# Layer norm by 32x32 tiles, a searched order for the attention and another step for Sobel, in a four-layer network

## The chip, the cores and the metric

The kernel runs on one core of one Trainium2 chip. Its time is device microseconds from start to end of one execution, given as a median of several runs. One execution is also recorded by the hardware profiler; PE is the matrix engine, PEld its weight loads, DVE the vector engine, ACT the scalar engine, POOL the GpSimd engine, and SP a queue that only issues DMAs.

## The reference

The input x is 256 x 256 positions of 32 channels, f32. Four layers follow, each `x = x + f(gn(x))`, where gn is a group norm over the whole picture (16 groups of 2 channels) without weights.

```
layer 0: mn = (m - mean) * rsqrt(var + eps) * gamma + beta     # over the 32 channels
         o  = sigmoid(mn @ Wg) * (mn @ Wv)                     # 32 -> 256
         return o @ Wo + bo                                    # 256 -> 32
layers 1, 2: pooled = 3x3 mean; sqrt(sobel_x(pooled)^2 + sobel_y(pooled)^2 + 1e-6)
layer 3: two recurrent cells of width 128 with group norm, over 256 steps of 256 sequences
```

In layer 0 the softmax is summed over the axis on which it was normalised, so that factor is 1 and queries and keys drop out; the kernel computes the two matmuls, the gate and the projection alone.

## The kernel before

The picture lies in SBUF as `xa`, 128 partitions x 64 blocks x 256: partition = position within a block (4, called j) x 32 channels, free = 256 rows. Work goes by pairs of blocks, 128 x 512 numbers; there are 32 pairs (`NST`), and `pair(t, k)` is pair k of tile t. `xb` is a second tile of the same shape.

**Input** (L205 to L222): 16 loads of 512 KB on SP's queue, 4 transposes a pair on PE, a copy on ACT (L221), bn_stats on DVE (L222). Three buffers of x hold two loads each. Then `group_norm` (L156) makes scale and bias of each partition by two small matmuls, with filler matmuls between.

**Layer norm, first half** (L262 to L276). For each pair PE multiplies `xa` by a centring matrix `cen` that also holds the group norm's scale (L264), ACT squares the result (L266), and DVE writes it, plus the constant `cb`, to `xb` (L267). Groups of four squares are averaged over the channels by 32-column matmuls into one bank, `pvar` (L254). One square root (L274) and one reciprocal (L276) give `rstd`, a row for each j and pair.

**Layer norm, second half** (L282 to L300). For each pair PE spreads its rows of `rstd` over the partitions (L285), DVE multiplies (L292), and ACT or POOL in turn applies gamma and beta (L294, L298).

**Attention** (L314 to L382). Each pair needs 16 matmuls (L324) with 32 rows of weights, 128 columns and 512 moving columns: two halves (u) x four j, for values and for gates; j chooses the strip of 32 rows. ACT takes the sigmoid of a gate (L339), DVE multiplies it with the value into a tile `o` (L342, 17 buffers). `project` runs 8 matmuls with all 128 rows and 32 columns into one bank (L348), ACT adds the output's bias (L356), POOL adds to `xa` (L358), and DVE takes bn_stats (L361). Values and gates have four PSUM banks each. The order is written out: `together` takes four values or gates of four different j, and the projection of a pair follows one pair later. In `manual_schedule` every engine keeps the order in which the program issues.

`RecurrentWeights` (L618) loads the cells' weights `wc` (2 x 512 KB) and `bc` on SP's queue; `centring` (L659) is a list of small DVE and POOL instructions on them, spread over the attention's pairs.

**Sobel** (L393), twice. For each pair: `convert` (ACT, L451), `twos` (DVE, L455), `threes` (DVE, L470), `ends` (ACT, L460), `fours`, `difference`, `smooth` (POOL, L475, L483, L479), two `mixed` of PE (L517), two `square` (ACT, L523), `total` (DVE, L527), `root` (ACT, L531), `residual` (DVE, L534), `statistics` (DVE, L537). Each part has a due time in `parts`; part p of pair k is due at `k * every + when`, and the parts are issued in the order of their due times. So `every` sets the order on each queue, not a time.

**Recurrence** (L840): 256 steps, from 604 us to the end.

The functions around the change, with the line numbers that the profile uses:

Of the kernel before, what the change touches and what calls it, by code (L numbers as in the profile page):

```python
# [18 lines left out]
S = 256  # L19
T = 256  # L20
# [41 lines left out]
def net_kernel(  # L62
# [69 lines left out]
    wg4 = four_times(w_g, D, "wg4")  # L132
    wo = cp.tile([P, D // P, C], F32, name="wo")
# [21 lines left out]
    def group_norm(stats, psum, before, after, rhs=None):  # L155
# [22 lines left out]
        return scale, bias  # L178

    KS = NST // 4  # L180


    means = ExitStack()
    mp = means.enter_context(tc.tile_pool(name="means", bufs=1))
    avg = mp.tile([P, KS, KS, J], F32, name="avg")
    nc.gpsimd.memset(avg, 0.0)
    for ks in range(KS):
        nc.gpsimd.tensor_copy(avg[:, ks, ks, :], kt[:, K_AVG, 0:P:C])
    spread = mp.tile([P, KS * J, C], F32, name="spread")
    for g in range(4):  # L190
        rows = slice(g * C, (g + 1) * C)
        nc.gpsimd.tensor_copy(
            spread[rows], ident[rows, rows].unsqueeze(2).to_broadcast([C, KS * J, C])
        )
# [6 lines left out]
    with tc.tile_pool(name="nat", bufs=3) as natp, tc.tile_pool(  # L201
# [3 lines left out]
        for w0 in range(0, T, WL):  # L205
            nat = natp.tile([P, 2, WL, C], F32, name="nat")
            for h in range(2):
                nc.sync.dma_start(out=nat[:, h], in_=x_nat[:, h, w0 : w0 + WL, :])
            for b2 in range(WL // (2 * J)):
# [14 lines left out]
        gn = group_norm(stats, ps_in, 3, 2, xa[:, NB - 1, :])  # L224

# [4 lines left out]

    pairs = [(g * KS + ks, g, ks) for ks in range(KS) for g in range(4)]

# [3 lines left out]
    with tc.tile_pool(name="ln", bufs=4) as lnp:  # L239
        rstd = lnp.tile([P, 2 * S], F32, name="rstd", bufs=1)  # L240
        with tc.tile_pool(name="ps_ln", bufs=6, space=PSUM) as ps_ln, tc.tile_pool(
            name="ps_var", bufs=1, space=PSUM
        ) as ps_var:
            cen = lnp.tile([P, P], F32, name="cen", bufs=1)
            nc.vector.tensor_scalar(cen, kg[:, K_CEN, :], gn[0], None, ALU.mult)
            pcb = ps_var.tile([P, 1], F32, name="pcb")
            nc.tensor.matmul(pcb, lhsT=kg[:, K_CEN, :], rhs=gn[1], start=True, stop=True)
            cb = lnp.tile([P, 1], F32, name="cb", bufs=1)
            nc.vector.tensor_copy(cb, pcb)
            pvar = ps_var.tile([P, 2 * S], F32, name="pvar")  # L250
            sqs = {}

            def variance(k, g, ks):
                nc.tensor.matmul(  # L254
                    pvar[g * C : (g + 1) * C, :],
                    lhsT=avg[:, ks].rearrange("p k j -> p (k j)"),
                    rhs=sqs.pop(k),
                    start=ks == 0,
                    stop=ks == KS - 1,
                )  # L260

            for i, (k, g, ks) in enumerate(pairs):  # L262
                pc = ps_ln.tile([P, 2 * S], F32, name="pc")
                nc.tensor.matmul(pc, lhsT=cen, rhs=pair(xa, k), start=True, stop=True)  # L264
                sqs[k] = lnp.tile([P, 2 * S], F32, name="sq", bufs=10)
                nc.scalar.activation(sqs[k], pc, AF.Square, bias=cb)  # L266
                nc.vector.tensor_scalar(pair(xb, k), pc, cb, None, ALU.add)  # L267
                if g == 3 and ks:
                    for q in pairs[i - 7 : i - 3]:
                        variance(*q)  # L270
            for q in pairs[-4:]:
                variance(*q)
            std = lnp.tile([P, 2 * S], F32, name="std", bufs=1)
            nc.scalar.activation(std, pvar, AF.Sqrt, bias=ln_eps)  # L274
            table(AF.Sigmoid, std[:, 0:1])
            nc.vector.reciprocal(rstd, std)  # L276
            for _ in range(9):
                nc.tensor.matmul(
                    pvar[:, 0:S], lhsT=ident, rhs=kg, start=True, stop=True
                )  # L280
        with tc.tile_pool(name="ps_sp", bufs=8, space=PSUM) as ps_sp:
            for i, (k, g, ks) in enumerate(pairs):  # L282
                rows = slice(g * C, (g + 1) * C)
                pb = ps_sp.tile([P, 2 * S], F32, name="pb")
                nc.tensor.matmul(  # L285
                    pb,
                    lhsT=spread[rows, ks * J : (ks + 1) * J, :].rearrange("p j c -> p (j c)"),
                    rhs=rstd[rows, :],
                    start=True,
                    stop=True,  # L290
                )
                nc.vector.tensor_mul(pair(xb, k), pair(xb, k), pb)  # L292
                if i % 2:
                    nc.scalar.activation(  # L294
                        pair(xb, k), pair(xb, k), AF.Identity, scale=gamma4, bias=beta4
                    )
                else:
                    nc.gpsimd.tensor_scalar(  # L298
                        pair(xb, k), pair(xb, k), gamma4, beta4, ALU.mult, ALU.add
                    )  # L300
            junk = ps_sp.tile([P, 2 * S], F32, name="pb")
            for _ in range(4):
                nc.tensor.matmul(
                    junk[:, 0:S], lhsT=ident, rhs=kg, start=True, stop=True
                )
# [4 lines left out]
    cells = ctx.enter_context(tc.tile_pool(name="cells", bufs=1))  # L310
    rw = RecurrentWeights(tc, cells, w_cell, b_cell)
    centring = rw.centring()
    stats = new_stats()
    with tc.tile_pool(name="at", bufs=3) as atp, tc.tile_pool(  # L314
        name="ps_g", bufs=4, space=PSUM
    ) as ps_g, tc.tile_pool(name="ps_v", bufs=4, space=PSUM) as ps_v:
        gates, gated = {}, {}

        def inner(w, u, j, ps):
            i, half = divmod(u, 2)  # L320
            k = pairs[i][0]
            rows = slice(j * C, (j + 1) * C)
            mn = xb[rows, 2 * k : 2 * k + 2, :].rearrange("p b s -> p (b s)")
            nc.tensor.matmul(  # L324
                ps, lhsT=w[rows, half * P : (half + 1) * P], rhs=mn, start=True, stop=True
            )
            return ps

        def together(values, gates_of):

            pvs = {k: inner(wv4, *k, ps_v.tile([P, 2 * S], F32, name="pv")) for k in values}
            pgs = {
                k: inner(wg4, *k, ps_g.tile([P, 2 * S], F32, name="pg"))
                for k in gates_of
                if k[0] < 2 * NST
            }
            for k, pg in pgs.items():
                gates[k] = sg = atp.tile([P, 2 * S], F32, name="sg", bufs=8)
                nc.scalar.activation(sg, pg, AF.Sigmoid)  # L339
            for k, pv in pvs.items():  # L340
                gated[k] = o = atp.tile([P, 2 * S], F32, name="o", bufs=17)
                nc.vector.tensor_mul(o, pv, gates.pop(k))  # L342

        def project(i):
            po = ps_g.tile([P, 2 * S], F32, name="pg")
            for half in range(2):
                for j in range(J):
                    nc.tensor.matmul(  # L348
                        po[j * C : (j + 1) * C, :],
                        lhsT=wo[:, half, :],  # L350
                        rhs=gated.pop((2 * i + half, j)),
                        start=half == 0,
                        stop=half == 1,
                    )
            r = atp.tile([P, 2 * S], F32, name="r", bufs=2)
            nc.scalar.activation(r, po, AF.Identity, bias=bo4)  # L356
            dst = pair(xa, pairs[i][0])
            nc.gpsimd.tensor_add(dst, dst, r)  # L358

        def statistics(i):  # L360
            nc.vector.bn_stats(stats[:, i, :], pair(xa, pairs[i][0]))  # L361

        with tc.manual_schedule():
            together((), [(0, j) for j in range(J)])
            together((), [(1, j) for j in range(2)])
            for i in range(NST):
                for u in (2 * i, 2 * i + 1):
                    if i >= 3 and u % 2:
                        statistics(i - 3)
                    together([(u, 0), (u, 1)], [(u + 1, 2), (u + 1, 3)])  # L370
                    together([(u, 2), (u, 3)], [(u + 2, 0), (u + 2, 1)])
                if i >= 1:
                    project(i - 1)
                if centring:
                    centring.pop(0)()
            for part in centring:
                part()
            table(AF.Sqrt, one)
            for i in range(NST - 1, NST):
                project(i)  # L380
            for i in range(NST - 3, NST):
                statistics(i)  # L382
# [740 lines left out]
```

## Time and profile before

| | |
|---|---|
| median of 3 runs | 2561.74 us (2558.74 to 2562.13) |
| profiled execution: time | 2562.2 us |
| profiled execution: span from first to last instruction | 2560.4 us |
| granted PE clock, mean | 0.991 |
| PE, DVE, ACT, POOL busy | 98%, 89%, 88%, 51% |

The stages, read from the first instructions of each: input to 34.9 us, group norm to 38.8, layer norm to 101.2, attention from 102.2 to 322.6, Sobel to 455.9 and to 592, and the recurrence from 604.

The page counts an engine as busy from start to end of each instruction, and for PE the end of a pass is modelled, so a full PE column need not be a full PE. Idle time is put down to the instruction that ended it. A group's line gives the line, the engine, the operation, output<-inputs, the shapes, the count, then busy us and the mean ns of one, then idle time before it. A line of the timeline gives start, length, engine, line, operation and count; the length covers all instructions of that line of the answer.

### The profile page before, as it was taken

To read this page: it belongs to the slowest core of one execution; us is meant where nothing else is said; L and a number is where in the kernel's file an instruction comes from. 1 tells how busy PE (TensorE), PEld (TensorE's weight loads), DVE (VectorE), ACT (ScalarE), POOL (GpSimd) and SP (SyncE) were. 2 spreads that over 40 slices of the span, in tenths; PEclk is the share of its full clock that TensorE was granted. 3 is DMA by queue.
4 is the path that set the end of the run, shared out by engine and by line. 5 is a ranking of instruction groups with operands and counts; after the bars stand their busy time and mean duration, and the time that the engine had idled before them with its cause. 6 is when DMAs were issued, how large, how long until landed. Compare 5 with 4: busy or idle time off the path is not lost.

```text
span 2560.4 us, 41317 instructions
## 1 busy us (share of the span) xinstructions
PE 2506.6 (98%) x11469; PEld 1048.9 (41%) x11469; DVE 2266.8 (89%) x6667; ACT 2247.8 (88%) x6888; POOL 1315.4 (51%) x1356
## 2 busy tenths in 40 slices
PE   7999999998999999999999999999999999999997
PEld 4433344544444444444444444444444444444442
DVE  6788877775999999999999999999999999999997
ACT  5677766575999999999999999999999999999997
POOL 3222277673555555555555555555555555555553
PEclk9899999998999999999999999999999999999998
DMA  4000000002010101010101010000101010100000
GB/s 150 17 1 1 1 1 1 1 1 50 5 21 5 21 5 22 5 22 5 22 5 22 5 24 10 19 18 9 22 5 22 5 22 5 22 5 5 5 5 11
DMA packets 110872, 38.57 MB, mean 15 GB/s; under 512 B 74868, under 2 KB 107797, under 8 KB 110632
## 3 DMA queue, kind: packets, MB, share of 16 engines
q1 hardware_dynamic: 108452, 34.54, 6.2%
q8 instruction: 94, 1.54, 0.3%
q14 instruction: 146, 1.20, 0.1%
q10 hardware_dynamic: 1380, 0.99, 0.1%
q0 software_dynamic: 800, 0.30, 0.0%
HBM read 10.63 MB, written 8.39 MB: 7 GB/s over the span
## 4 chain that ended last, share of the span: by engine, by line
PE 88%; DVE 6%; ACT 2%; issue 2%; DMA 1%; POOL 0%; SPq 0%; POOLq 0%; DVEq 0%; ACTq 0%
PE zz L941 36%; PE zz L936 17%; PE zz L909 9%; PE pt L993 5%; PE pv L324 5%; PE zz L906 3%; PE pg L348 2%; PE pt L989 2%; PE pg L517 2%; ACT pg L531 1%; PE px L1038 1%; DVE pp L470 1%; PE pg L324 1%; DVE ss L527 1%; DVE u L455 1%
## 5 line engine op out<-in xcount | busy, mean ns | idle before, releaser
L957 POOL TENSOR_TENSOR rs<-ve,mhalf 128x4 f32<-128x4 f32 x1024 | 1031.9, 1008 | 925.1 <-DVE ve L954 925.1
L941 PE MATMUL zz<-wc,hT 128*128 128x512 f32 x2040 | 1059.4, 607 | 0.7 <-DVE hT L999 0.7
L930 ACT ACTIVATE ga<-zz,rs 128x128 f32<-128x128 f32 x3072 | 975.6, 378 | 38.7 <-POOL rs L957 10.2
L954 DVE TENSOR_REDUCE ve<-sq 128x4 f32<-128x516 f32 x1024 | 705.0, 688 | 29.5 <-ACT sq L949 8.5
L949 ACT ACTIVATE sq<-zz 128x512 f32<-128x512 f32 x1024 | 632.2, 617 | 37.4 <-PE zz L941 16.1
L936 PE MATMUL zz<-wc,hT 128*128 128x512 f32 x1024 | 525.0, 594 | 0.0
L941 PEld LDWEIGHTS zz<-wc,hT 128*128 128x128 f32 x2040 | 328.8, 190 | 399.1 <-DVE c L985 167.6
L930 ACT ACTIVATE go<-zz,rs 128x128 f32<-128x128 f32 x1024 | 395.0, 386 | 0.0
L977 DVE TENSOR_TENSOR c<-ga 128x128 f32<-128x128 f32 x1024 | 300.2, 293 | 62.5 <-ACT ga L930 29.8
L985 DVE TENSOR_TENSOR c<-c,fc 128x128 f32<-128x128 f32 x1020 | 288.5, 283 | 9.0
L981 DVE TENSOR_TENSOR fc<-ga,c 128x128 f32<-128x128 f32 x1020 | 292.5, 287 | 2.7 <-ACT ga L930 2.7
L909 PE MATMUL zz<-fx,xt 32*128 32x512 f32 x2048 | 266.0, 589 | 0.0
L342 DVE TENSOR_TENSOR o<-pv,sg 128x512 f32<-128x512 f32 x256 | 158.2, 681 | 39.7 <-PE pg L324 34.6
L993 PEld LDWEIGHTS pt<-ident,c 128*128 128x128 f32 x512 | 71.1, 139 | 286.0 <-DVE c L985 277.0
L996 ACT ACTIVATE th<-c 128x128 f32<-128x128 f32 x512 | 166.7, 326 | 0.4 <-DVE c L985 0.4
L339 ACT ACTIVATE sg<-pg 128x512 f32<-128x512 f32 x256 | 138.6, 599 | 31.6 <-PE pg L324 26.8
L517 PE MATMUL pg<-dh,kt 128*64 128x512 f32 (+1 forms) x584 | 156.5, 542 | 7.4 <-POOL dh L483 6.3
L996 ACT ACTIVATE th<-pt 128x128 f32<-128x128 f32 x512 | 146.4, 286 | 18.8 <-PE pt L993 18.8
L936 PEld LDWEIGHTS zz<-wc,hT 128*128 128x128 f32 x1024 | 161.3, 197 | 2.8 <-issue 0.5
L999 DVE TENSOR_TENSOR hT<-pt,th 128x128 f32<-128x128 f32 x512 | 146.4, 286 | 15.9 <-ACT th L996 15.7
L324 PE MATMUL pv<-xb,wv 32*128 32x512 f32 x512 | 156.7, 619 | 0.0
L989 PEld LDWEIGHTS pt<-ident,go 128*128 128x128 f32 x512 | 71.4, 140 | 204.1 <-ACT go L930 203.6
(173 smaller groups left out, 2943.0 us busy)
## 6 DMA issues: line engine op xcount, KB each, us to landing
xt<-xa SPq DMA_DIRECT2D x256, 64.0 KB, 2.0
nat<-in_x_dram SPq DMA_DIRECT2D x16, 512.0 KB, 7.7
out_dram<-st SPq DMA_DIRECT2D x252, 32.0 KB, 1.7
wc<-in_L_conv_W_cell_dram SPq DMA_DIRECT2D x2, 512.0 KB, 4.5
kt<-in_consts_dram ACTq DMA_DIRECT2D x1, 704.0 KB, 7.0
kg<-in_consts_dram ACTq DMA_DIRECT2D x1, 128.0 KB
wv<-in_L_conv_Wv_dram POOLq DMA_DIRECT2D x4, 32.0 KB, 4.5
wg<-in_L_conv_Wg_dram POOLq DMA_DIRECT2D x4, 32.0 KB, 6.5
```

The costliest lines, as they stand in the source:

```text
L324: nc.tensor.matmul(ps, lhsT=w[rows, half * P : (half + 1) * P], rhs=mn, start=True, stop=True)
L909: nc.tensor.matmul(v["zz", l, h, t], lhsT=inputs.of(t, r), rhs=fx[r, :], start=False, stop=l == 0 and t == 0,)
L930: nc.scalar.activation(dst, gates(x, g), func, scale=scale)
L936: nc.tensor.matmul(get("zz"), lhsT=v["hT", 0, t][:, seqs], rhs=wc[:, l, 0, :], start=False, stop=t == 0)
L941: nc.tensor.matmul(get("zz"), lhsT=v["hT", l, t - 1][:, seqs], rhs=wc[:, l, 1, :], start=False, stop=True,)
L949: nc.scalar.activation(sqs[l, h, t % 2][:, :, 0:H], four(get("zz")), AF.Square, scale=float(H**-0.5))
L954: nc.vector.tensor_reduce(ve, sqs[l, h, t % 2], AX.X, ALU.add)
L957: nc.gpsimd.tensor_tensor(rs, get("ve"), inputs.mhalf, ALU.pow)
L977: nc.vector.tensor_mul(c, gates(get("ga"), 0), gates(get("ga"), 2))
L981: nc.vector.tensor_mul(fc, gates(get("ga"), 1), get("c"))
L985: nc.vector.tensor_add(c, c, get("fc"))
L996: nc.scalar.activation(th, get("pt")[:, 1, 0:P] if turned else get("c"), AF.Tanh)
```

## The change

It does three things.

**Sobel**: `every` is 3.6 instead of 3.44. The due times are the same, so the order of the parts on ACT and DVE changes: `total` goes behind `threes` of a later pair, `ends` behind the squares.

**Layer norm**: DVE and POOL in turn subtract the mean of the group norm from `xa` into `xb`, before the group's scale is known. PE centres with 16 matmuls of 32 x 32 a group of four pairs, ACT squares without a bias, and the centred values are not kept. The channels' centring matrix, gamma and the group's scale are multiplied into the attention's weights, beta becomes a bias of values and gates (`wbias`). Of the second half only the multiplication with `rstd` is left: for the first three pairs by matmul and DVE, for the other 29 by a DMA that repeats the row over 32 partitions, and POOL, three of them ahead and 26 within the attention.

**Attention**: the order is a list of due times with a step of 6.6 a pair, all eight PSUM banks are one pool in the order of release, `o` has 14 buffers and `sg` 7, sigmoid and multiplication take a bias, and the last pair's sum is one DVE instruction. `cells` is opened earlier, so the weights' buffers no longer wait for freed memory.

```diff
--- before.py
+++ after.py
-        return scale, bias
+        return scale, bias, mean
+    cells = ctx.enter_context(tc.tile_pool(name="cells", bufs=1))
...
+            if w0 == T - WL:
+                pbias = ps_in.tile([P, 2, 2, P], F32, name="pt")
...
+                nc.scalar.copy(wbias, pbias[:, :, :, 0:1].rearrange("p i h o -> p i (h o)"))
+                for w in (wv4, wg4):
+                    nc.gpsimd.tensor_scalar(w, w, gamma4, None, ALU.mult)
+                    pw = ps_in.tile([P, 2, 2, P], F32, name="pt")
+                    pw = pw[:, 0].rearrange("p h s -> p (h s)")
+                    nc.tensor.matmul(pw, lhsT=kg[:, K_CEN, :], rhs=w, start=True, stop=True)
+                    nc.scalar.copy(w, pw)
...
+        less = small.tile([P, 1], F32, name="less")
+        nc.vector.tensor_scalar_mul(less, gn[2], -1.0)
+        for w in (wv4, wg4):
+            nc.scalar.activation(w, w, AF.Copy, scale=gn[0])
+    def rows_of(k):
+        t = lnp.tile([P, 2 * S], F32, name="rows", bufs=4)
+        for j in range(J):
+            nc.sync.dma_start(
+                out=t[j * C : (j + 1) * C, :],
+                in_=rstd[j * C + k : j * C + k + 1, :].unsqueeze(1).to_broadcast([1, C, 2 * S]),
+            )
+        return t
+    def scaled(k):
+        nc.gpsimd.tensor_mul(pair(xb, k), pair(xb, k), rowsets.pop(k))
...
-            for i, (k, g, ks) in enumerate(pairs):
-                pc = ps_ln.tile([P, 2 * S], F32, name="pc")
-                nc.tensor.matmul(pc, lhsT=cen, rhs=pair(xa, k), start=True, stop=True)
-                sqs[k] = lnp.tile([P, 2 * S], F32, name="sq", bufs=10)
-                nc.scalar.activation(sqs[k], pc, AF.Square, bias=cb)
-                nc.vector.tensor_scalar(pair(xb, k), pc, cb, None, ALU.add)
+            for k in range(NST):
+                e = nc.gpsimd if k % 2 else nc.vector
+                e.tensor_scalar(pair(xb, k), pair(xa, k), one, less, ALU.mult, ALU.add)
+            for g in range(GROUPS):
+                pcs = [ps_ln.tile([P, 2 * S], F32, name="pc") for _ in range(J)]
+                for j in range(J):
+                    rows = slice(j * C, (j + 1) * C)
+                    for r in range(J):
+                        nc.tensor.matmul(
+                            pcs[j][r * C : (r + 1) * C, :],
+                            lhsT=cen[rows, rows],
+                            rhs=pair(xb, J * g + r)[rows],
...
+                for pc in pcs:
+                    sqs.append(lnq.tile([P, 2 * S], F32, name="sq"))
+                    nc.scalar.activation(sqs[-1], pc, AF.Square)
+                if g:
+                    variance(g - 1, last)
...
+            for k in range(FIRST, FIRST + 4):
+                rowsets[k] = rows_of(k)
+            for k in range(FIRST):
+                pb = ps_sp.tile([P, 2 * S], F32, name="pb")
+                nc.tensor.matmul(pb, lhsT=spread[:, k, :], rhs=rstd, start=True, stop=True)
+                nc.vector.tensor_mul(pair(xb, k), pair(xb, k), pb)
+            for k in range(FIRST, FIRST + 3):
+                scaled(k)
...
+    step = 6.6
+    plan = [
+        (0.00, "g", 0, 3), (0.69, "g", 1, 2), (0.71, "sg", 0, 3), (2.04, "sg", 1, 2),
+        (2.73, "g", 0, 2), (3.75, "v", 1, 3), (3.82, "g", 0, 0), (4.63, "sg", 0, 2),
+        (5.07, "sg", 0, 0), (5.18, "v", 0, 2), (6.86, "g", 1, 3), (6.90, "mu", 0, 2),
+        (8.48, "v", 0, 3), (8.51, "v", 0, 0), (8.95, "sg", 1, 3), (8.97, "g", 0, 1),
+        (9.39, "mu", 1, 3), (9.68, "mu", 0, 3), (9.83, "sg", 0, 1), (10.81, "mu", 0, 0),
+        (10.94, "v", 1, 2), (11.35, "v", 1, 0), (11.96, "mu", 1, 2), (12.63, "g", 1, 1),
+        (13.03, "sg", 1, 1), (13.09, "v", 0, 1), (13.24, "v", 1, 1), (13.90, "g", 1, 0),
+        (14.15, "sg", 1, 0), (14.62, "mu", 1, 1), (14.89, "mu", 0, 1), (15.03, "mu", 1, 0),
+        (20.69, "pr", 0, 0), (22.72, "r", 0, 0), (27.37, "bn", 0, 0),
+    ]
...
+                sg = sbuf["sg", u, j, k] = atp.tile([P, 2 * S], F32, name="sg", bufs=7)
+                nc.scalar.activation(sg, held["g", u, j, k][1], AF.Sigmoid, bias=bias(1))
+                release(("g", u, j, k))
+            elif o == "mu":
+                gated = sbuf["o", u, j, k] = atp.tile([P, 2 * S], F32, name="o", bufs=14)
+                nc.vector.scalar_tensor_tensor(
+                    gated, held["v", u, j, k][1], bias(0), sbuf.pop(("sg", u, j, k)), ALU.add, ALU.mult,
+                )
+                release(("v", u, j, k))
...
+        def take(key):
+            n = free.pop(0)
+            held[key] = n, ps_at.tile([P, 2 * S], F32, name="pa", tag=f"bank{n}")
+            return held[key][1]
+        def release(key):
+            free.append(held.pop(key)[0])
+        todo = [
+            (k * step + when, one_of, (o, u, j, k)) for k in range(NST) for when, o, u, j in plan
+        ]
+        for k in range(first, NST):
+            at = (k - first) * step
+            todo.append((at + 4.0, scaled, (k,)))
+            if k > first:
+                todo.append((at - step + 0.5, spread_out, (k,)))
...
-        every = 3.44
+        every = 3.6
```

Some lists of the diff are set closer here; nothing in them is changed. The new lines that the prediction names: the weights' chain L221 to L234, the subtractions L288, the 32x32 matmuls L306, the variance L292, the gate and value matmuls L393, the sigmoid L402, the gated multiply L406, the projection L419, the residual of Sobel L620.

## The prediction

> **What bounds the kernel now.** I read the stage table first, because the change touches only the first 592 us.
>
> ```profile
> core 0: us, PE busy (x) PEld busy (x) DVE busy (x) ACT busy (x) POOL busy (x), PEclk, DMA share, GB/s
> 38.80:75.70 36.90, 36.75 (x128) 12.94 (x128) 23.97 (x33) 21.93 (x33) 0.00 (x0) 1.00 0.00 1
> 80.60:101.20 20.60, 20.58 (x71) 12.96 (x72) 19.22 (x32) 12.36 (x16) 12.29 (x16) 0.69 0.07 23
> 114.00:308.00 194.00, 194.00 (x1396) 72.53 (x1397) 160.62 (x267) 145.74 (x262) 49.59 (x51) 1.00 0.00 1
> 322.70:455.90 133.20, 126.57 (x633) 60.02 (x632) 100.97 (x168) 86.79 (x163) 97.35 (x98) 1.00 0.01 1
> 604.00:2560.40 1956.40, 1934.55 (x8248) 784.62 (x8244) 1807.57 (x5912) 1852.00 (x6176) 1031.89 (x1024) 0.99 0.07 13
> ```
>
> The layer norm's first half (38.8 to 75.7) is full on PE; its second (80.6 to 101.2) nearly full on DVE. The recurrence, 1956 us, is untouched. PE's busy time includes passes that only overlap, so the pace is read from the chain of waits, in order of time:
>
> ```profile
> 38.81 7.10 PE pc L264 x16
> 45.91 1.00 PE pvar L254 x8
> ...
> 81.80 17.42 DVE xb L292 x29
> ...
> 208.73 1.85 PE pg L348 x16
> ```
>
> A full f32 matmul of 512 columns is two passes of 0.444 (16 in 7.10). Four matmuls on four column strips of 32 share them (16 passes in 1.85, 0.116 each). The second half of the layer norm is 29 multiplies at 0.60 start to start. Attention repeats every 6.69 us (L348 starts at 208.73 and again at 215.41). For Sobel and the attention loop the timeline gives single instructions:
>
> ```profile
> 379.96 0.68 DVE L527 TENSOR_TENSOR ss<-sq,pg 128x512 f32<-128x512 f32 x1
> 380.49 2.27 PE L517 MATMUL pg<-dh,kt 128*64 128x512 f32 x8
> 380.67 0.69 ACT L531 ACTIVATE pg<-ss,sobel_eps 128x512 f32<-128x512 f32 x1 [1.15 <-DVE ss L527]
> 381.39 0.69 DVE L534 TENSOR_TENSOR xb<-xa,pg 128x512 f32<-128x512 f32 x1 [0.76 <-ACT pg L531]
> 382.22 2.26 PE L517 MATMUL pg<-sh,kt 128*64 128x512 f32 x8
> ...
> 217.20 0.70 PE L324 MATMUL pv<-xb,wv 32*128 32x512 f32 x2
> 217.73 0.59 PE L324 MATMUL pv<-xb,wv 32*128 32x512 f32 x2
> 218.43 2.48 DVE L342 TENSOR_TENSOR o<-pv,sg 128x512 f32<-128x512 f32 x4 [1.22 <-PE pg L324]
> ```
>
> Sobel's loop lies between DVE and ACT: total (L527) to root 0.71, root to residual 0.72, then residual, threes, statistics and twos on DVE 0.61 + 0.59 + 0.60 + 0.59, in all 3.82 us a pair. Its PE runs 8 passes in 1.73 (380.49 to 382.22), 3.45 a pair: little is spare. In attention a matmul on one 32-row strip is two passes, 0.43 to 0.53 apart, and its reader starts 1.23 after its first pass.
>
> **The change, part by part**, against the profiled execution (span 2560.4, time 2562.2, 0.5 above the median 2561.74). Line numbers of new code are those of the changed kernel. Four stages move by tens of microseconds.
>
> Input and statistics, +3. In the built order SP sends the two wc loads (1.05 MB) behind the first six loads of x, ahead of the other ten. The load stage moves 344 to 410 GB/s at a DMA share near 1, so x lands 2.6 to 3.0 later; the last transposes waited 1.3 on ACT, not on a DMA, so 1.3 to 1.7 remains. The weights' chain (L221 to L234: PE, two POOL multiplies near 0.7 each, PE, ACT) stands ahead of the last chunk's transposes in PE's queue, 1.5 to 2 us, and runs during that wait for x. A reduction (bm, 0.67) moves ahead of bn_aggr on DVE, in the chain: +0.7. In the group norm `less` (0.16) and three subtractions (L288) go between q and cen on DVE; at 0.4 to 0.7 each, less the 0.78 for which DVE waited for std, +0.5 to +1. Bounds +1 to +5.
>
> Layer norm, first half, -15. L288's 16 DVE and 16 POOL instructions run ahead (POOL's nearest row, L298, is 0.77, so a group each 1.54). PE now runs 16 matmuls of 32x32 a group. Row strips run four at once in the trace (L285: 8 passes in 1.18) and so do column strips (L348). Both together is not shown: between all 16 at once (2 x 0.43 = 0.9) and the 32-column row's pace (32 x 0.116 = 3.7). I take 16, since strips of each kind already run apart. With the variance's 1.0 and a switch of shape a group costs 2.2, against ACT's four squares at 0.49 without a bias, 1.96. Eight groups are 17.6, head and last variance 2.8, and 1.6 for POOL (two-input rows vary from 1.04, L475, to 1.27, L358: 0.2 x 8): 22 for 36.9, so -15. The other end, 8 x 4.9 + 1.7 = 41, is +4. [...]
>
> Layer norm, second half, -18. From the end of the variance to the first gate matmul it was 75.67 to 102.16 = 26.5. Now: std 0.69, reciprocal 3.35, fillers on PE until 4.9, three spread matmuls one after the other (5 passes of 0.43 to the last, 0.7 to its reader), one multiply 0.75: 8.5. The first gate matmul waits for DVE's third multiply. The scales of the other 29 pairs are spread by 116 DMAs on SP's queue (64 KB from SBUF landed in 2.0 us in the xt rows; four sets at once, then one a pair, with nothing urgent behind them), and POOL's multiply (nearest L358, 1.27) is early by several pairs. Per pair POOL then has 1.27 + 1.27 + 0.6 of more than 6 us: free.
>
> Attention, +38. Sigmoid gains a bias: 0.60 becomes 0.69 by L356, 9 x 0.59 = 5.3 of ACT a pair. The gated multiply becomes L406 with a pointer bias: L267 starts every 0.67 against 0.60, so DVE needs 8 x 0.67 + 0.60 = 6.0. Neither reaches 6.69. The order does. Following the built program's waits from one pair to the next: the projection's first matmul frees a gated buffer (14 now, 17 before), on which `mu` (1,1) waits: 1.13 after the projection starts. Then two more multiplies, 0.69 + 0.68, and the third's end frees a bank, 0.77. Into it goes g(0,2), and behind it v(1,2) and v(0,2), all on row strip 2, so one after the other: 0.86 + 0.85. The last is read 1.15 later (1.23 without the switch's 0.1), its multiply frees a bank after 0.77, g(1,0) runs there 0.97 with the switch to full rows, and only then comes the next projection. Sum 7.87 us against 6.69, x 32 = +38. The old order never put two matmuls in a row on one strip. Bounds: 7.4 (every release 0.05 faster) to 8.3, +23 to +52.
>
> Sobel, -19. With 3.6 `total` moves behind `threes`, and `twos` and the rest fill the root's time: DVE's loop is 0.71 + 0.72 + 0.61 + 0.59 + 0.60 = 3.23. What is late next is PE at 3.45. (3.82 - 3.45) x about 26 steady pairs x 2 layers = 19. Bounds: step 3.6 to 3.82 holds, -11 to 0; PE without a gap, -22.
>
> Sum: +3 - 15 - 18 + 38 - 19 = -11: 2562.2 - 11 = 2551.
>
> **Rivals.**
> 1. Slower: the 32x32 tiles run at the 32-column pace. Speaks for it: 0.116 a pass is the only measured pace of 32-column matmuls; against: four such passes start within 0.05 us. Layer norm +4 instead of -15: 2570. A group above 4.3 us decides for slower by 0.2%.
> 2. Attention runs at its step of 6.6 or less, because the strips do not queue or the buffer is free earlier: -3 instead of +38, 2510. Speaks for it: DVE's 6.0 and ACT's 5.3 allow it; against: 0.43 a pass is what 512 columns take in every row.
> 3. Sobel's new order does not do what it should, PE or POOL (3 x 1.0) holds it at 3.75 or more: -4 instead of -19, 2566, no change. Against: PE's 1.73 per eight passes.
> 4. Nothing of the layer norm counts because the clock, 0.69 in 80.6 to 101.2, sinks there: PE's 2.2 becomes 3.2, +8, 2559.
>
> **How the numbers follow.** Mine 64%, rival 1 14%, rival 2 9%, rival 3 8%, rival 4 5%. About 0.2% (5 us) is what a measurement tells from no change. My case's own range is 2540 to 2563: four fifths of it are faster, the rest the same. Faster: 0.51 + 0.09 + some of the fourth = 0.62. Same: 0.13 + 0.07 + 0.03 = 0.21. Slower: rival 1 and the upper ends, 0.17. Predicted 2551; range 2534 to 2569 leaves out rival 2 and the top of rival 1.
>
> **What would show it.** Right: 22 us between cen and std; first gate matmul 8 to 9 us behind the variance; the projection (L419) every 7.6 to 8.1 us, with `mu` waiting for PE's projection and v(0,2) behind two others of its strip; residuals (L620) every 3.4 to 3.5 with PE full. Wrong: projections every 6.6, or groups of the layer norm above 4 us.

## The result and the profile after

The changed kernel takes 2569.35 us (median of 8 runs, 2567.85 to 2571.38) against 2561.82 of the kernel before (8 runs): a ratio of 1.0031, with an interval of 1.002 to 1.0041. It is slower by 7.5 us, where the prediction had 2551, 11 us gained, and a range up to 2569.0. The profiled execution of the changed kernel took 2571.4 us (span 2569.3), 9.2 more than the profiled execution before, and the balance below is made between these two.

The stage table of the changed kernel has the same columns as that of before: the stretch and its length, busy time and count of PE, weight loads, DVE, ACT and POOL, the granted clock, the DMA share and GB/s. The rows are the end of the group norm, the two halves of the layer norm, the attention, and both Sobel layers.

```profile
core 0: us, PE busy (x) PEld busy (x) DVE busy (x) ACT busy (x) POOL busy (x), PEclk, DMA share, GB/s
38.80:45.43 6.63, 4.00 (x19) 3.20 (x20) 5.84 (x14) 2.75 (x5) 3.08 (x4) 0.95 0.01 2
45.43:67.12 21.69, 21.65 (x320) 5.04 (x320) 11.10 (x13) 16.42 (x33) 11.73 (x13) 0.86 0.01 3
67.12:75.36 8.24, 6.73 (x24) 4.48 (x24) 5.42 (x4) 2.26 (x3) 0.00 (x0) 1.00 0.33 11
75.36:348.30 272.94, 262.30 (x1536) 122.39 (x1536) 199.71 (x296) 186.07 (x289) 89.74 (x89) 0.98 0.51 29
348.30:601.30 253.00, 246.68 (x1275) 143.77 (x1275) 216.90 (x335) 176.33 (x331) 195.53 (x206) 0.99 0.02 5
```

| stage | before, us | after, us | difference | predicted |
|---|---|---|---|---|
| start to the first matmul of the layer norm | 38.8 | 45.4 | +6.6 | +3 |
| layer norm, first half | 36.9 | 21.7 | -15.2 | -15 |
| layer norm, second half | 26.5 | 8.2 | -18.3 | -18 |
| attention | 220.4 | 272.9 | +52.5 | +38 |
| two Sobel layers | 269.4 | 253.0 | -16.4 | -19 |

The five differences add up to +9.2. The layer norm came out as worked out, Sobel nearly; the attention lost 14.5 us more than its price, and that alone turns -11 into a loss.

The chain of waits of the changed kernel, in order of time (start, length, what), shows a group of the layer norm and then the place where the extra attention time lies:

```profile
54.00 1.16 PE pc L306 x32
55.17 1.00 PE pvar L292 x8
56.16 1.16 PE pc L306 x32
...
97.09 1.29 POOL xb L279
...
101.35 6.09 DMA rows<-rstd
...
107.60 1.26 POOL xb L279
108.86 1.23 POOL xa L435
...
110.72 0.74 DVE o L406
...
305.11 1.85 PE pa L419 x16
306.96 6.15 PE pa L393 x31
313.12 1.85 PE pa L419 x16
```

A group of the layer norm is 2.16 us: the sixteen 32x32 matmuls, 32 passes, take 1.16. From 97 to 111 the chain runs through POOL and a DMA, in an attention that had been PE's. And the projection repeats every 8.01 us (305.11, 313.12), where 7.87 had been predicted and 6.69 was measured before.

The timeline of POOL and then of DVE at that place tells who stood behind whom; the bracket is the idle time before an instruction and what ended it.

```profile
97.09 1.28 POOL L279 TENSOR_TENSOR xb<-xb,rows 128x512 f32<-128x512 f32 x1 [4.52 <-DVE o L406]
102.36 1.26 POOL L279 TENSOR_TENSOR xb<-xb,rows 128x512 f32<-128x512 f32 x1 [3.99 <-PE pa L419]
107.60 1.26 POOL L279 TENSOR_TENSOR xb<-xb,rows 128x512 f32<-128x512 f32 x1 [3.97 <-DMA rows<-rstd]
108.82 1.26 POOL L435 TENSOR_TENSOR xa<-xa,r 128x512 f32<-128x512 f32 x1
...
110.11 0.69 DVE L438 BATCH_NORM_STATS2 stats<-xa 128x6 f32<-128x512 f32 x1 [10.83 <-POOL xa L435]
```

The multiplications by rstd (L279) come every 5.25 us. The projection of pair 0 ran at 92.45, but its sum (L435) stands on POOL behind the multiplication of pair 8, which by the plan is due at 17.2 while the sum is due at 22.7; pair 8's rows land at 107.4. DVE had the statistics of pair 0 (L438) next, idled 10.83 us for that sum, and all gated multiplies behind it waited, so banks stayed full and PE stood idle for 8.15 us, up to its matmul at 111.51.

### The profile page after: what moved, and what is told of

Same layout as the page of the kernel before. It is cut to its first block, busy times and chain, and to the rows that moved or that the text cites. A ratio compares the mean times of both kernels' runs of the same rounds, so it can differ in the third digit from the quotient of the medians.

```text
span 2569.3 us, 41531 instructions
## 1 busy us (share of the span) xinstructions
PE 2510.2 (98%) x11605; PEld 1094.3 (43%) x11605; DVE 2274.3 (89%) x6623; ACT 2254.0 (88%) x6876; POOL 1350.1 (53%) x1387
## 3 DMA queue, kind: packets, MB, share of 16 engines
q8 instruction: 95, 1.56, 0.2%
## 4 chain that ended last, share of the span: by engine, by line
PE 96%; DMA 1%; DVE 1%; issue 1%; ACT 1%; POOL 0%; SPq 0%; DVEq 0%; POOLq 0%; ACTq 0%
PE zz L1027 36%; PE zz L1022 17%; PE zz L995 9%; PE pg L603 8%; PE pa L393 8%; PE pt L1079 5%; PE zz L992 3%; PE pa L419 2%; PE pt L1075 2%; PE px L1124 1%; PE px L1114 1%; PE pg L516 1%; DMA nat<-in_x_dram 1%; PE pc L306 0%; PE pvar L292 0%
## 5 line engine op out<-in xcount | busy, mean ns | idle before, releaser
L402 ACT ACTIVATE sg<-pa,wbias 128x512 f32<-128x512 f32 x256 | 168.9, 687 | 89.5 <-PE pa L393 47.7
L406 DVE SCALAR_TENSOR_TENSOR o<-pa,wbias,sg 128x512 f32<-128x512 f32 x256 | 177.5, 746 | 60.5 <-PE pa L419 46.2
L393 PE MATMUL pa<-xb,wv 32*128 32x512 f32 x512 | 181.3, 615 | 8.7 <-DVE o L406 8.1
L393 PE MATMUL pa<-xb,wg 32*128 32x512 f32 x512 | 171.3, 638 | 0.8 <-DVE xb L335 0.8
```

The source lines that it names most:

```text
L393: nc.tensor.matmul(take((o, u, j, k)), lhsT=w[rows, u * P : (u + 1) * P], rhs=pair(xb, k)[rows], start=True, stop=True,)
```

## The experiments

The theory formed on this trace: the stall comes from the order on POOL together with slow row DMAs; the period of 8.01 comes from the searched order, through the loop over a gated buffer, as predicted; the missing 3.6 us at the input come from the weights' chain in PE's queue. The rivals are given with each run. Each ratio is to the kernel before, run beside it. Its median was 2562.07 us beside Sobel alone, POOL's multiplications later, products in place and the first of the early gammas; 2564.84 beside the rows from 32 partitions, the old order, the one without the bias and the one with the projection between the halves; and 2562.12 beside the old order's repetition and its early gamma.

### Sobel alone

```diff
-        every = 3.44
+        every = 3.6
```

> The kernel before with Sobel's step 3.6 instead of 3.44 and nothing else. Theory (the order of total and threes is what held a pair at 3.82, and PE at 3.45 is next): residuals every 3.4 to 3.5, about 26 steady pairs in each of two layers, -17 us: 2545. Rival (the gain seen in the changed kernel needs its other edits): no change, 2562.

Measured: 2540.61 us, ratio 0.9917 (0.9902 to 0.9932), 17 to 25 us less. The two lines of the residual give its first and last start in each layer, this kernel:

```profile
L534 DVE TENSOR_TENSOR xb<-xa,pg x32: 686/686/690, 341.0 to 446.9; 128x512 f32<-128x512 f32 x32
L534 DVE TENSOR_TENSOR xa<-xb,pg x32: 686/686/689, 464.8 to 574.0; 128x512 f32<-128x512 f32 x32
```

105.9 and 109.2 us for 31 steps, 3.42 and 3.52 on average; the same line of before ran 339.3 to 454.5 and 472.5 to 590.1, 3.72 and 3.79 with the ends of the layers. The step alone, in the old kernel, brings the gain; the other edits have no part in it. In the trace 16 us of it lie in Sobel, as in the changed kernel (the last residual starts at 574.0 against 590.1).

### POOL's multiplications later

```diff
-            todo.append((at + 4.0, scaled, (k,)))
+            todo.append((at + 20.0, scaled, (k,)))
```

> The changed kernel with POOL's multiplications by rstd inside the attention due 16 units (2.4 pairs) later, so that they stand behind the first pairs' sums in POOL's queue; DMAs and their sizes are unchanged. Theory (the stall of 10.8 us at 100 to 111 is an order: the sum of pair 0 stands on POOL behind the multiplication of pair 8, which waits for its rows, and DVE's statistics of pair 0 wait for that sum ahead of the gated multiplies): the stall goes, -10 us, 2559. Rival (the rows come too slowly, 5.25 us a pair, for any order): the wait moves to the first matmuls of pairs 6 to 9, 2567 to 2570.

Measured: 2558.27 us, ratio 0.9984 (0.9975 to 0.9993): 11 us below the changed kernel, and now faster than before by a hair. The row DMAs are as slow as they were (a median of 6.2 us to landing against 6.4). In this kernel's timeline the sum of pair 0 follows the first multiplication of the attention:

```profile
95.31 1.27 POOL L279 TENSOR_TENSOR xb<-xb,rows 128x512 f32<-128x512 f32 x1 [4.43 <-PE pa L393]
96.54 1.27 POOL L435 TENSOR_TENSOR xa<-xa,r 128x512 f32<-128x512 f32 x1
```

The theory holds: what cost 11 us was an order on one engine's queue. The rows come every 5.1 to 5.3 us (L279 at 95.31, 100.62 and 105.70) and a pair needs 8, so here the supply was enough once the urgent work stood in front.

### Rows from 32 partitions

```diff
-                in_=rstd[j * C + k : j * C + k + 1, :].unsqueeze(1).to_broadcast([1, C, 2 * S]),
+                in_=rstd[j * C : (j + 1) * C, :],
```

> The changed kernel with each of the 116 row DMAs reading 32 different partitions of rstd instead of one partition 32 times: the same bytes, the same count, the same queue and order. It leaves out the right scale (values of the layer norm are wrong). Theory (one source partition is what limits a row DMA to 64 KB in 1.31 us): landing in about 2 us like the xt loads, no wait of POOL for rows, and the stall at 100 to 111 gone, -10 us, 2559. Rival (bytes written, descriptors or the queue limit it): 64 KB each 1.3 us as before and 2569.

Measured: 2560.25 us, ratio 0.9986 (0.9975 to 0.9996), again 11 us below the changed kernel's ratio, with POOL's order untouched. The line of the row DMAs' time from issue to landing, changed kernel first, then this one:

```profile
DMA to landing us min/median/max: 4.7/6.4/8.0
```

```profile
DMA to landing us min/median/max: 1.9/2.0/3.6
```

And the window of 90 to 100 us of each, in which the DMA share and GB/s are the last two columns:

```profile
90.00:100.00 10.00, 10.00 (x62) 5.05 (x60) 6.82 (x11) 7.18 (x12) 2.54 (x2) 1.00 0.84 48
```

```profile
90.00:100.00 10.00, 10.00 (x66) 4.12 (x64) 6.88 (x11) 6.47 (x10) 3.08 (x3) 1.00 0.35 80
```

The same bytes, at 48 GB/s with the DMA engines 84% busy, or at 80 with 35%. One source partition read 32 times is what makes a set of rows take 5.25 us. So the stall needed two things, slow rows and the order on POOL, and taking away either removes it.

While rows were moved without a break (75 to 120 us), the changed kernel's DMA moved 45 to 52 GB/s.

### Products in place

```diff
-                sg = sbuf["sg", u, j, k] = atp.tile([P, 2 * S], F32, name="sg", bufs=7)
+                sg = sbuf["sg", u, j, k] = atp.tile([P, 2 * S], F32, name="o", bufs=21)
...
-                gated = sbuf["o", u, j, k] = atp.tile([P, 2 * S], F32, name="o", bufs=14)
+                gated = sbuf["o", u, j, k] = sbuf["sg", u, j, k]
```

> The changed kernel with the gated product written over its sigmoid: one set of 21 buffers instead of 14 and 7, the order of all instructions unchanged. Theory (the projection that frees a gated buffer is part of the loop that sets the period): 8.01 falls to 7.0, 32 x 1.0 = -32 us, 2537. Rival (row strips and the eight banks alone set the period): 7.9 to 8.0, 2566 to 2569.

Measured: 2545.86 us, ratio 0.9938 (0.9923 to 0.9953), 23.5 us below the changed kernel. What DVE waited for between 120 and 290 us, the changed kernel first, then this one (engine, line, waited for: us in total, times, longest):

```profile
DVE o L406 <- PE pa L419: 33.4, 21, 1.6
DVE o L406 <- PE pa L393: 2.8, 16, 0.2
```

```profile
DVE o L406 <- ACT o L402: 16.1, 24, 0.8
DVE o L406 <- PE pa L393: 6.6, 37, 0.5
```

In the changed kernel a gated multiply waits 1.6 us for the projection once in each pair; with the products in place that wait is gone. Two projections of this kernel's chain, five pairs apart, give the period:

```profile
262.13 1.85 PE pa L419 x16
...
297.80 1.85 PE pa L419 x16
```

It is 7.13, so 0.88 less a pair; the buffer was part of the loop, as the prediction said. The expectation of 32 us was too high: the period fell less, and the pairs ahead of the stall, which this kernel still has, gain nothing.

### Gamma into the centring matrix

```diff
+    gcen = mp.tile([P, P], F32, name="gcen")
+    nc.gpsimd.tensor_scalar(gcen, kg[:, K_CEN, :], gamma4, None, ALU.mult)
...
-                    nc.gpsimd.tensor_scalar(w, w, gamma4, None, ALU.mult)
...
-                    nc.tensor.matmul(pw, lhsT=kg[:, K_CEN, :], rhs=w, start=True, stop=True)
+                    nc.tensor.matmul(pw, lhsT=gcen, rhs=w, start=True, stop=True)
```

> The changed kernel with gamma multiplied into the centring matrix early on POOL instead of into the two weight tiles late, so that the two matmuls of the weights' chain wait for nothing in PE's queue. Theory (the chain held the last transposes 3.2 us, of which POOL's two multiplications are 1.9): -2 us, 2567. Rival (x itself lands later because the cells' weights are loaded ahead of it, and the chain only fills that wait): no change, 2569.

The same edit was also made on the next kernel, the one in the old order, and that kernel run beside it:

> The old order with gamma multiplied into the centring matrix early, one POOL instruction instead of two, and the two matmuls of the weights' chain without a wait. Theory (the chain holds the last transposes, and POOL's part of it is 1.9 of its 3.2 us): 1.5 to 2.5 us below the kernel without this edit on the same chip. Rival (x sets the time and the chain is hidden): within 0.5 us.

> The kernel in the old order once more, to be compared on the same chip with the next one: ratio to before 0.984.

Measured: 2569.1 us, ratio 1.0026 (1.0017 to 1.0035) for the first, against 1.0031 without the edit; 2518.59 (0.9832, 0.9818 to 0.9845) against 2520.32 (0.9834, 0.982 to 0.9848) for the second pair. Both times 1 to 2 us less, both times within the intervals: the times don't settle it. The traces show what it was about. PE at the input, changed kernel:

```profile
29.81 1.64 PE L240 MATMUL pt<-ident,nat 128*128 128x128 f32 x13 [0.16 <-ACT xa L247]
31.38 0.60 PE L221 MATMUL pt<-beta,wv 32*128 32x1 f32 x4
...
33.16 0.70 PE L233 MATMUL pt<-wv,kg 128*128 128x256 f32 x2 [0.73 <-POOL wv L230]
34.06 0.80 PE L233 MATMUL pt<-wg,kg 128*128 128x256 f32 x2 [0.21 <-POOL wg L230]
34.65 3.52 PE L240 MATMUL pt<-ident,nat 128*128 128x128 f32 x16
```

The last 16 transposes start 3.3 us after the first matmul of the chain, and in all this time PE waits for ACT or POOL, never for a load. With the edit the same stretch is 1.95 us (31.85 to 33.80). So the chain does hold the transposes, and POOL's share of it is 1.3 us; the x that was to hide it had landed. What this is worth in time, 1 to 2 us, stays unproven.

### The old order of the attention

```diff
-        todo = [(k * step + when, one_of, (o, u, j, k)) for k in range(NST) for when, o, u, j in plan]
+            for i in range(NST):
+                if ahead < NST and i + 3 >= ahead:
+                    ...
+                    scaled(ahead)
+                for u in (2 * i, 2 * i + 1):
+                    if i >= 3 and u % 2:
+                        statistics(i - 3)
+                    together([(u, 0), (u, 1)], [(u + 1, 2), (u + 1, 3)])
+                    together([(u, 2), (u, 3)], [(u + 2, 0), (u + 2, 1)])
+                if i >= 1:
+                    project(i - 1)
```

`together` and `project` are those of the kernel before, with the biases of the changed one and the products in place.

> The changed kernel with the attention in the order of the kernel before (four values or gates of four strips at a time, banks in two sets of four, project one pair later), with the bias in sigmoid and multiplication, products in place in 21 buffers, and each later multiplication by rstd on POOL three pairs ahead of its use. Theory (the searched order is what costs; the bias has a small price in the loop): period 6.95 instead of 8.01 and no stall, -40 us, 2529. Rival 1 (the bias or the row DMAs hold the attention, whatever the order): 7.8 or more, 2560. Rival 2 (bias is hidden, as the prediction had it): 6.69, -48, 2521.

Measured: 2522.76 us, ratio 0.984 (0.9824 to 0.9857); the repetition above gave 0.9834. That is 41 us, 1.6%, below the kernel before, and the fastest way found here, with or without the early gamma. Two projections of this kernel in its chain of waits, one pair apart:

```profile
281.54 1.85 PE pg L377 x16
288.46 1.85 PE pg L377 x16
```

The period is 6.92, 1.1 us a pair below the changed kernel. That row DMAs or bias as such hold the attention at 8 is out. But the 1.1 is not the price of the order alone, because this kernel also has the products in place and its banks in two sets of four. The searched order with the products in place had 7.13, so 0.9 of the 1.1 came with the buffers, and 0.2 is left for the order and the banks. The old order with bias and 14 and 7 buffers was not run. Against the searched order with the products in place the time is 25 us less (0.984 against 0.9938); about 11 of that is the stall, which this kernel does not have, and some 7 are the 0.2 a pair.

### Without the bias

```diff
-                nc.scalar.activation(sg, pg, AF.Sigmoid, bias=wbias[:, 1, h : h + 1])
+                nc.scalar.activation(sg, pg, AF.Sigmoid)
...
-                nc.vector.scalar_tensor_tensor(o, pv, wbias[:, 0, h : h + 1], o, ALU.add, ALU.mult)
+                nc.vector.tensor_mul(o, pv, o)
```

> The kernel in the old order of this same call without the bias of sigmoid and multiplication; it leaves out beta. Theory (each bias lengthens instructions in the loop of banks: 0.07 on DVE and 0.09 on ACT, several times a pair): 6.68 instead of 6.95, -8 us against the old order with bias. Rival (DVE's 6.0 and ACT's 5.3 a pair leave room, the bias is hidden): the same time within 2 us.

Measured: 2516.32 us, ratio 0.9811 (0.9795 to 0.9827), 6 to 7 us below the kernel with bias. The same two lines:

```profile
275.30 1.85 PE pg L377 x16
281.99 1.85 PE pg L377 x16
```

6.69, exactly the period before. So the biases cost 0.23 us a pair in this order, though DVE's 6.0 us and ACT's 5.3 a pair, the prediction's estimates, lie below either period, and DVE idles 0.97 us in each pair. The rival, a hidden bias, is out. The cost fits the theory that both instructions are links of the loop that frees the banks, which was not followed link by link here.

### The projection between the halves

```diff
+                    if u % 2 and i >= 1: project(i - 1)
...
-                if i >= 1:
-                    project(i - 1)
```

> The kernel in the old order with the projection issued between the two halves of a pair, and gamma multiplied into the centring matrix early. Theory: period 6.9 and 2 us less at the input: 2527. Rival (the projection there stands behind multiplies that are not done, and PE waits): 7.2 or more, 2537.

This kernel has the early gamma too. Measured: 2524.67 us, ratio 0.9842 (0.9826 to 0.9858), no better than the old order with the early gamma (0.9832) or without it. The period is 7.02, not 6.9 as forecast, so moving the projection did not help; the rival's 7.2 did not come either.

## Why the prediction was wrong, point by point

- **Input, +3 predicted, +6.6 measured.** The step that failed is that the weights' chain "runs during that wait for x". After 24 us PE waited for no load (they ran at 413 GB/s from 25 to 30 us). ACT's copies of the last two chunks of x (L247), and those of the kernel before (L221), show where the time went:

```profile
30.51 2.05 ACT L247 COPY xa<-pt 128x512 f32<-128x512 f32 x4 [0.75 <-PE pt L240]
...
36.18 1.86 ACT L247 COPY xa<-pt 128x512 f32<-128x512 f32 x3 [0.91 <-PE pt L240]
```

```profile
28.99 2.05 ACT L221 COPY xa<-pt 128x512 f32<-128x512 f32 x4 [0.75 <-PE pt L214]
31.79 2.05 ACT L221 COPY xa<-pt 128x512 f32<-128x512 f32 x4 [0.75 <-PE pt L214]
```

  The chunk ahead of the chain is 1.5 us late, inside the 1.3 to 1.7 foreseen. The last chunk is 4.4 late: the chain, 3.3 us where 1.5 to 2 were foreseen (POOL's two multiplications took 0.93 and 0.91 where "near 0.7" had been put), came on top of the late x and did not hide in it. The end of bn_stats is 4.6 late, and from there to the first matmul of the layer norm it is +2.0 (5.9 against 3.9), of which 1.2 to 1.7 were foreseen. That the 1.5 comes from the hoisted wc loads was not tried by itself.
- **Layer norm, first half, -15 and -15.2.** All 16 at once was right: 32 passes in 1.16 us are 0.036 each, against 0.116 with column strips alone; rival 1 is out. POOL was not late: its subtractions took 0.93 beside DVE's at 0.99, so a group of four had its input in 1.9 us, where the nearest row before (L298) had given 1.54. That the sum came out so close is in part luck: the 1.6 set aside for POOL was not needed, and a low clock took about 2 us instead (last section).
- **Layer norm, second half, -18 and -18.3.** First gate matmul 8.2 us behind the variance, 8.5 predicted.
- **Attention, +38 and +52.5.** The loop was right where it was checked. Without the gated buffer in it the period fell by 0.88. In the steady part the projection starts at 208.95, the waiting multiply at 210.03 (1.08 against 1.13), and v(0,2), which the order puts behind two matmuls of its strip, is multiplied last, at 215.10:

```profile
210.03 4.89 DVE L406 SCALAR_TENSOR_TENSOR o<-pa,wbias,sg 128x512 f32<-128x512 f32 x7 [1.59 <-PE pa L419]
215.10 0.75 DVE L406 SCALAR_TENSOR_TENSOR o<-pa,wbias,sg 128x512 f32<-128x512 f32 x1 [0.17 <-PE pa L393]
```

  The period is 8.01 for 7.87, +4 us over 32 pairs. The step that failed lies in the other part: the rows were taken as landing in 2.0 us "with nothing urgent behind them", and POOL as free because its multiply "is early by several pairs". The 2.0 us came from the xt loads, which read 32 partitions; a row DMA, which reads one, takes 6.4 to land, and sets follow each other every 5.25. And what is urgent does not stand behind the DMAs on SP but behind the multiplication on POOL: the sum of pair 0, then the statistics on DVE, then every gated multiply. That cost 10.8 us, more than half of the 20 between the forecast and the difference of the two profiles. With slow rows, being early was the fault: what is issued early stands in POOL's queue ahead of what is needed.
- **Sobel, -19 and -16.4.** The order does what the loop said; steady pairs run at 3.41 to 3.45, on PE. The term was a little large because the ends of the layers don't gain.
- **"Neither reaches 6.69"** was right for the bound of DVE and ACT, but the bias was not free in the old order: 0.23 a pair.
- Of the rivals none came true as priced: rival 4's lower clock came, but took some 2 us (last section). The loss came by a mechanism that was costed at nothing. In the chances, the three terms given for no change (0.13 + 0.07 + 0.03) make 0.23, not 0.21.

## What to carry to other kernels

When work is moved to an engine that has time to spare, list what stands behind it in that engine's queue, not only whether its sum of busy time fits: here POOL was 33% busy in the attention and still stopped everything for 11 us. Take a DMA's duration from a row with the same source pattern; the same 64 KB took 2.0 us to land with 32 partitions read and 6.4 with one. A searched order should be read for its loops, with buffers and instruction lengths in them, before its step is believed: a step of 6.6 in the list ran at 8.0, and at 7.1 once the gated buffer was out of its loop; a plain order written by hand, with the same buffers, ran at 6.9.

## What the runs showed of the hardware

The granted clock at the start of the layer norm differs from run to run of nearly the same code: 0.50 and 1.00 in the two windows below. The first windows of the 32x32 matmuls, in the changed kernel and then in the one with POOL's multiplications later:

```profile
45.43:49.00 3.57, 3.57 (x62) 1.27 (x64) 3.57 (x5) 1.51 (x4) 3.57 (x5) 0.50 0.03 7
```

```profile
45.80:49.40 3.60, 3.56 (x71) 1.31 (x72) 3.60 (x5) 2.37 (x5) 3.60 (x5) 1.00 0.03 7
```

In both PE is idle for 2.5 us ahead of the first such matmul, and 2.5 to 2.6 in five of the profiles; two of the five begin at 0.50 and 0.54 (the early gamma), three at 1.00. In the five profiles of the old order four filler matmuls stand later, the gap is 1.56 to 1.58 us, and the clock is 1.00 in each. At 0.50 the first two groups took 4.6 us instead of 2.9, and the half 21.7 against 19.6 in the old order's profile. With POOL's multiplications later, whose code up to there is that of the changed kernel, the first row DMA is issued 23.8 us behind the first such matmul (69.6 and 45.84); in the old order it is 23.7 (68.1 and 44.38), in the changed kernel 25.8 (71.2 and 45.43). So some 2 us of the layer norm's time came from a start that these kernels don't set, and without them the half would have beaten the forecast by 2 us. Whether the shorter gap keeps the clock up is not shown: five profiles of each kind are few.

DVE and POOL subtracted side by side, both from SBUF to SBUF (L288). On DVE an instruction took 0.99 us at the median and 0.54 at its fastest; the two at 0.54 (42.28 and 45.19) began within 0.1 us of one on POOL that took 1.03 or 1.02. On POOL the median was 0.93, where the nearest row before had 0.77 (L298). One after the other, 0.54 and 0.77 would be 1.31, an estimate that takes L298's time for POOL's; in the steady part (46.2 to 54 us) each engine began one every 0.91 to 0.92. What L288 takes on either engine with the other idle is not shown.
